# Moving the transposes of layer 1's rows from TensorE to 32x32 block transposes on VectorE

## The chip, the cores and the metric

The kernel runs on one core of one Trainium2 chip. The metric is the device time of that core in microseconds (us), from the first instruction to the last, as a median over several executions. Engines are named as the profile names them: PE is TensorE (PEld its weight loads), DVE is VectorE, ACT is ScalarE, POOL is GpSimd, SPq the DMA queue that SyncE feeds.

## The reference, cut to what matters

The input x has 16 batch elements of 1024 rows and 256 channels in float32. Two graph layers follow each other.

```python
def _batchnorm(x, gamma, beta):                      # over all 16 x 1024 rows
    return (x - mean(x, 0)) * rsqrt(var(x, 0) + EPS) * gamma + beta

# layer 0: aggregation over the graph, a two-layer perceptron with two batch norms
out = relu(_batchnorm(agg @ W1.T + b1, g1, be1)) @ W2.T + b2
x = _layernorm(x + _batchnorm(out, g2, be2))
# layer 1: a graph gate makes q; k and v are linear; 4 heads of 64 channels
attn = softmax(einsum('bhnd,bhmd->bhnm', q, k) * scale)
x = _layernorm(x + einsum('bhnm,bhmd->bhnd', attn, v))
```

The second batch norm needs the statistics of all rows, so its input (called y) goes to DRAM. It comes back when layer 1 begins with a batch element. The kernel computes y with channels on partitions; the residual and the layer norm want rows on partitions. Somewhere y must be transposed.

## The kernel before

Layer 1 is a software pipeline. While the scores, exponentials and weighted sums of one batch element run, the rows of later ones are prepared in small pieces, a pair of 128-row tiles (b, j) at a time: load, batch norm (`bn2`), transpose with residual and statistics (`ln1_a`), normalization (`ln1_b`), transpose of the result (`x1_t`).

```python
def fetch_rows(b, j):
    nc.sync.dma_start(yts[b, j], yT_dram[b][:, :, ts(j, 2 * P)])
    nc.sync.dma_start(xrs[b, j], x[b, ts(j, 2 * P), :].rearrange("(a p) c -> p a c", p=P))
...
def bn2(b, j):
    for c in range(CT):
        t = yts[b, j][:, c, :]
        nc.scalar.activation(t, t, AF.Identity, bias=t2[:, c : c + 1], scale=s2[:, c : c + 1])
...
def ln1_a(b, j):
    p = ps_t.tile([P, 2, C], F32, tag="t", name="py")
    for a in range(2):
        for c in range(CT):
            nc.tensor.transpose(p[:, a, ts(c, P)], yts[b, j][:, c, ts(a, P)], ident)
    x1s[b, j] = x1p.tile([P, 2, C], F32, tag="x1", name=f"x1_{b}_{j}")
    nc.vector.tensor_add(x1s[b, j], p, xrs[b, j])
    mvs[b, j] = ln_stats(sm, x1s[b, j], f"a{b}_{j}")
```

VectorE also adds up the exponentials (`sums`). When all are in, TensorE sums the result over partitions into the denominators of the softmax (`dens`, tile pd):

```python
def sums(g):
    ...
        for a in range(2):
            nc.vector.tensor_add(ACC[b, hf, pair], ACC[b, hf, pair], E[g, a])
def dens(b, hf):
    p = ps_t.tile([P, FB], F32, tag="t", name="pd")
    for pair in range(NP):
        acc = ACC.pop((b, hf, pair))
        for h in range(2):
            k = 32 * (2 * pair + h)
            nc.tensor.matmul(p[k : k + 32, :], ones32, acc[:, h, :], start=True, stop=True)
```

A small scheduler puts each piece into a half-bundle (`put`), and `arrange` orders the pieces of a half-bundle. The denominators and the batch norm come first there:

```python
order = (dens, recips, finish_a, finish_b, x1_t, ln1_a, ln1_b, means, load, crow)
short = (dens, recips, finish_a, x1_t, ln1_a, crow)
def arrange(pieces):
    first = [fa for fa in pieces if fa[0] is dens]
    ...
    first += [fa for fa in pieces if fa[0] is bn2]
    ...
    return first + flat
```

One period of this pipeline is one batch element: two halves (hf) of two head pairs each, so four bundles of pieces, each followed by four steps of scores and sums.

## Time and profile before

| what | before |
|---|---|
| time, median of 4 executions | 2586.84 us |
| TensorE busy in the profiled execution | 2514.0 of 2584.4 us (97%) |
| TensorE waits of pd for VectorE's sums | 2.6 us in 9 |
| TensorE waits of the scores for an exponential | 19.6 us in 16 |
| transposes that the change removes | 60 groups of four, 0.43 us each |

A row of the view of waits names an engine and a line of the kernel, what it waited for, and then the total in us, the number of waits and the longest.

```profile
PE s L686 <- ACT e L698: 19.6, 16, 4.1
...
PE pd L738 <- DVE acc L707: 2.6, 9, 0.3
```

In the timeline the columns are start, duration, engine, line, operation, output and inputs, count.

```profile
1333.86 7.89 DVE L707 TENSOR_TENSOR acc<-acc,e 128x1024 f32<-128x1024 f32 x6
```

Six sums take 7.9 us when nothing disturbs them.

### The profile page before, as it was taken

How to read it: one execution, taken by the hardware profiler on the slowest of the kernel's cores; microseconds unless marked ns; L12 is line 12 of the kernel's file. 1: busy time of each engine (PE TensorE's matmuls, PEld its weight loads, DVE VectorE, ACT ScalarE, POOL GpSimd, SP SyncE). 2: the span in 40 equal slices, each digit the busy share in tenths (PEclk: the TensorE clock that was granted, in tenths of full speed). 3: DMA queues.
4: the chain of work that ended last, by engine and by line, in shares of the span. 5: the costliest groups of instructions: out<-in, count | busy, mean ns of one | idle time of the engine just before them, and what ended most of it. 6: DMA issues, size and time to landing. Idle time of an engine off the chain costs nothing.

```text
span 2584.4 us, 33296 instructions
## 1 busy us (share of the span) xinstructions
PE 2514.0 (97%) x13053; PEld 1092.5 (42%) x13053; DVE 1650.8 (64%) x2588; ACT 1135.0 (44%) x1509; POOL 565.7 (22%) x588
## 2 busy tenths in 40 slices
PE   8999999998997999999999999999999999999997
PEld 4444444443443544344444444444444444443432
DVE  5555555456676676675766757666576675766666
ACT  2000000004543656465564655646556465564644
POOL 2222222223654011011110111201121110211112
PEclk9999999999998999999999999999999999999998
DMA  3122221230873101101011010110101100010000
GB/s 130 73 90 82 98 98 66 98 130 30 329 302 129 41 21 54 34 25 34 29 54 34 25 33 30 54 33 25 34 25 58 34 25 34 25 53 22 9 9 26
DMA packets 94115, 163.77 MB, mean 63 GB/s; under 512 B 7688, under 2 KB 73856, under 8 KB 86784
## 3 DMA queue, kind: packets, MB, share of 16 engines
q1 hardware_dynamic: 93952, 161.57, 17.8%
q8 instruction: 105, 1.72, 0.3%
q14 instruction: 58, 0.48, 0.1%
HBM read 98.58 MB, written 62.98 MB: 63 GB/s over the span
## 4 chain that ended last, share of the span: by engine, by line
PE 87%; ACT 7%; DVE 3%; issue 1%; DMA 1%; POOL 0%; SPq 0%; DVEq 0%; ACTq 0%; POOLq 0%
PE s L686 15%; PE o L717 15%; PE pg L660 14%; PE pa L295 14%; PE po L457 7%; PE ph L326 7%; PE pk L635 4%; PE pv L646 2%; DVE acc L707 2%; PE pd L738 1%; ACT e L698 1%; PE px L585 1%; PE pa L276 1%; ACT wg L623 1%; ACT wg L622 1%
## 5 line engine op out<-in xcount | busy, mean ns | idle before, releaser
L698 ACT ACTIVATE e<-s 128x1024 f32<-128x1024 f32 x512 | 496.0, 1020 | 378.1 <-PE s L686 331.1
L707 DVE TENSOR_TENSOR acc<-acc,e 128x1024 f32<-128x1024 f32 x384 | 470.7, 1226 | 94.5 <-ACT e L698 66.3
L686 PE MATMUL s<-qT,kT 64*64 64x512 f32 x4096 | 491.6, 595 | 20.3 <-ACT e L698 19.6
L717 PE MATMUL o<-e,v 64*64 64x512 f32 x4096 | 486.1, 590 | 0.0
L660 PE MATMUL pg<-wg,x 128*128 128x512 f32 x960 | 437.6, 593 | 0.0
L686 PEld LDWEIGHTS s<-qT,kT 64*64 64x64 f32 x4096 | 147.0, 133 | 315.3 <-issue 252.1
L717 PEld LDWEIGHTS o<-e,v 64*64 64x64 f32 x4096 | 156.9, 133 | 284.2 <-issue 278.6
L66 POOL TENSOR_SCALAR rs_z<-mv_z 128x2 f32<-128x2 f32 x64 | 41.0, 641 | 1046.1 <-DVE mv_z L519 963.2
L627 DVE SCALAR_TENSOR_TENSOR wg<-wg,adj_sb 128x1024 f32<-128x1024 f32 x128 | 156.8, 1225 | 127.6 <-ACT wg L623 125.4
L660 PEld LDWEIGHTS pg<-wg,x 128*128 128x128 f32 x960 | 170.1, 190 | 159.2 <-issue 159.1
L93 ACT COPY u<-pa 128x512 f32<-128x512 f32 x15 | 8.8, 585 | 475.3 <-PE pa L295 475.3
L295 PE MATMUL pa<-AhT,x 128*128 128x512 f32 x360 | 161.8, 592 | 0.0
L668 DVE TENSOR_TENSOR qT<-pg,para_sb 128x512 f32<-128x512 f32 x64 | 44.2, 691 | 168.0 <-PE pg L660 167.0
L66 POOL TENSOR_SCALAR rs_a<-mv_a 128x2 f32<-128x2 f32 x64 | 43.0, 671 | 415.3 <-DVE mv_a L519 413.9
L586 ACT COPY x1T<-px 128x512 f32<-128x512 f32 x64 | 37.1, 581 | 202.5 <-PE px L585 202.5
L646 PE MATMUL pv<-kvw,x1T 128*128 128x256 f32 x512 | 120.1, 379 | 0.0
L635 PE MATMUL pk<-x1T,kvw 128*128 128x512 f32 x256 | 118.9, 609 | 0.7 <-ACT x1T L586 0.7
L326 PE MATMUL ph<-agg,SW 128*128 128x512 f32 x240 | 112.8, 592 | 0.0
L729 DVE TENSOR_TENSOR ot<-o,ot 128x512 f32<-128x512 f32 x64 | 44.1, 689 | 102.3 <-ACT ot L728 102.3
L295 PE MATMUL pa<-T,sx 128*128 128x512 f32 x240 | 107.9, 592 | 0.0
L295 PEld LDWEIGHTS pa<-AhT,x 128*128 128x128 f32 x360 | 68.4, 190 | 86.1 <-issue 86.1
L646 PEld LDWEIGHTS pv<-kvw,x1T 128*128 128x128 f32 x512 | 94.0, 190 | 17.9 <-issue 7.4
(188 smaller groups left out, 3258.1 us busy)
## 6 DMA issues: line engine op xcount, KB each, us to landing
h<-hT SPq DMA_DIRECT2D x28, 1024.0 KB, 4.4
hL<-h SPq DMA_DIRECT2D x28, 1024.0 KB, 9.8
x<-in_x_dram SPq DMA_DIRECT2D x16, 1024.0 KB, 7.3
yT<-y SPq DMA_DIRECT2D x32, 512.0 KB, 3.2
out_dram<-r SPq DMA_DIRECT2D x64, 256.0 KB, 2.1
yt<-yT SPq DMA_DIRECT2D x62, 256.0 KB, 3.4
xr<-in_x_dram SPq DMA_DIRECT2D x62, 256.0 KB, 5.0
crow<-crow_d SPq DMA_DIRECT2D x15, 512.0 KB, 4.1
```

The lines of the kernel that those rows point to most:

```text
L66: nc.gpsimd.tensor_scalar(dst, src, add, None, op0=OP.add)
L295: nc.tensor.matmul(p, xs[n][:, k, :], bs[n][:, k, :], start=(k == 0), stop=(k == KN - 1))
L326: nc.tensor.matmul(p, ws[n][:, ts(f, P)], bs[n], start=True, stop=True)
L457: nc.tensor.matmul(p, ws[n][:, k, :], bs[n][:, k, :], start=(k == 0), stop=(k == KF - 1))
L627: nc.vector.scalar_tensor_tensor(t, t, 1.0, adj_sb[:, i, :], op0=OP.add, op1=OP.mult)
L635: nc.tensor.matmul(p, kvw[:, k, ts(c, P)], x1Ts[b][:, k, ts(h, FB)], start=(k == 0), stop=(k == CT - 1))
L646: nc.tensor.matmul(p[:, ts(a, C)], x1Ts[b][:, k, ts(j + a, P)], kvw[:, k, C:], start=(k == 0), stop=(k == CT - 1),)
L660: nc.tensor.matmul(pg[b], x1s[b, k // 2][:, k % 2, ts(c, P)], wgs[b, k][:, ts(h, FB)], start=(k == 0), stop=(k == NT - 1))
L686: nc.tensor.matmul(t[r * HD : (r + 1) * HD, h, :], kTs[b, pair][h * HD : (h + 1) * HD, ts(2 * cb + r, HD)], qTs[b, pair, hf][h * HD : (h + ...
L698: nc.scalar.activation(E[g, a], S.pop((g, a)), AF.Exp)
L707: nc.vector.tensor_add(ACC[b, hf, pair], ACC[b, hf, pair], E[g, a])
L717: nc.tensor.matmul(O[b, hf, pair][r][h * HD : (h + 1) * HD, :], vs[b][r * HD : (r + 1) * HD, cb, pair * P + h * HD : pair * P + (h + 1) * HD],
```

## The change

Its intent: take the transposes, 1% of TensorE's work, away from the engine that bounds the kernel. y is laid out in DRAM so that a DMA can fetch 32x32 blocks, already put where they belong as blocks; VectorE's block transpose then turns each block. Batch norm now needs a different constant for each block of columns, and goes with the residual to GpSimd, which is idle for 78% of the span (busy 565.7 of 2584.4 us). Batch element 0 keeps the old way.

```diff
+    Q = 32
+    NQ = P // Q
+    y_blk = [yT_all[b].rearrange("i (d e) (q n) -> q e (i d) n", e=Q, q=NQ) for b in range(B)]
...
         def fetch_rows(b, j):
-            nc.sync.dma_start(yts[b, j], yT_dram[b][:, :, ts(j, 2 * P)])
+            if b == 0:
...
+            else:
+                for q in range(NQ):
+                    nc.sync.dma_start(
+                        yts[b, j][q * Q : (q + 1) * Q].rearrange("p a (d n) -> p (a d) n", n=Q),
+                        y_blk[b][q][:, ts(j, 2 * C // Q), :],
+                    )
...
+        def bn2_q(b, j):
+            y = yts[b, j].rearrange("p a (d n) -> p a d n", n=Q)
+            for k, op in enumerate((OP.mult, OP.add)):
+                sc = stq[:, k, :].unsqueeze(1).unsqueeze(3).to_broadcast([P, 2, C // Q, Q])
+                nc.gpsimd.tensor_tensor(y, y, sc, op)
+
+        def rows(b, j):
+            x1s[b, j] = x1p.tile([P, 2, C], F32, tag="x1", name=f"x1_{b}_{j}")
+            nc.vector.transpose(x1s[b, j].rearrange("p a c -> p (a c)"), yts[b, j].rearrange("p a c -> p (a c)"))
+            nc.gpsimd.tensor_add(x1s[b, j], x1s[b, j], xrs[b, j])
...
-                put(b - 2, j + 1, bn2, b, j)
+                put(b - 2, j + 1, bn2_q, b, j)
+                put(b - 2, j + 2, rows, b, j)
                 put(b - 2, j + 2, ln1_a, b, j)
...
-        order = (dens, recips, finish_a, finish_b, x1_t, ln1_a, ln1_b, means, load, crow)
+        order = (dens, recips, finish_a, rows, finish_b, x1_t, ln1_b, ln1_a, means, load, crow)
-        short = (dens, recips, finish_a, x1_t, ln1_a, crow)
+        short = (dens, recips, finish_a, x1_t, crow)
```

For b > 0 `ln1_a` now holds the statistics alone. Cut here: the new layout's stores, the round trip of the constants through DRAM into `stq`, a buffer count of 5 instead of 6 for small tiles, and the kernel's fallback path.

More of the change, by code (lines that the diff above doesn't have):

```diff
@@ L75, in load_vec @@
         return t
-    yT_all = dram.tile([B, P, CT, N], F32, name="yT")
-    yT_dram = [yT_all[b] for b in range(B)]
+    yT_all = dram.tile([B, NT, C, P], F32, name="yT")
+    y_chunk = [[yT_all[b][:, ts(c, P), :].rearrange("i p n -> p i n") for c in range(CT)] for b in range(B)]
+    Q = 32
+    NQ = P // Q
+    y_blk = [yT_all[b].rearrange("i (d e) (q n) -> q e (i d) n", e=Q, q=NQ) for b in range(B)]
+    st2_dram = dram.tile([2, C], F32, name="st2_d")
     c_dram = [dram.tile([NT, P], F32, name=f"crow_d{b}") for b in range(B)]
@@ L390, in gnn_norm_attention_kernel @@
         ones32 = keep.tile([P, 32], F32, name="ones32")
+        stq = keep.tile([P, 2, C // Q], F32, name="stq")
         nc.gpsimd.memset(ones32, 1.0)
@@ L409, in load @@
         def load(b, j):
-            yts[b, j] = ldp.tile([P, CT, 2 * P], F32, tag="yt", name=f"yt{b}_{j}")
+            shape = [P, CT, 2 * P] if b == 0 else [P, 2, C]
+            yts[b, j] = ldp.tile(shape, F32, tag="yt", name=f"yt{b}_{j}")
             xrs[b, j] = ldp.tile([P, 2, C], F32, tag="xr", name=f"xr{b}_{j}")
@@ L414, in fetch_rows @@
         def fetch_rows(b, j):
-            nc.sync.dma_start(yts[b, j], yT_dram[b][:, :, ts(j, 2 * P)])
+            if b == 0:
+                for c in range(CT):
+                    nc.sync.dma_start(
+                        yts[b, j][:, c, :].rearrange("p (a n) -> p a n", n=P), y_chunk[b][c][:, ts(j, 2), :]
+                    )
+            else:
+                for q in range(NQ):
+                    nc.sync.dma_start(
+                        yts[b, j][q * Q : (q + 1) * Q].rearrange("p a (d n) -> p (a d) n", n=Q),
+                        y_blk[b][q][:, ts(j, 2 * C // Q), :],
+                    )
             nc.sync.dma_start(xrs[b, j], x[b, ts(j, 2 * P), :].rearrange("(a p) c -> p a c", p=P))
@@ L474, in second @@
                     if k >= 5:
-                        nc.sync.dma_start(yT_dram[b][:, :, ts(k - 5, FB)], ys[k - 5])
+                        for c in range(CT):
+                            nc.sync.dma_start(
+                                y_chunk[b][c][:, ts(k - 5, FB // P), :],
+                                ys[k - 5][:, c, :].rearrange("p (i n) -> p i n", n=P),
+                            )
                         if k == 6:
@@ L538, in fast @@
         otp = pool("otp", 3)
-        sm = pool("sm", 6)
+        sm = pool("sm", 5)
         rp = pool("rp", 2)
@@ L552, in bn2, with constants_q @@
                 nc.scalar.activation(t, t, AF.Identity, bias=t2[:, c : c + 1], scale=s2[:, c : c + 1])
+        def constants_q():
+            with nc.allow_non_contiguous_dma(reason="a few hundred numbers"):
+                for k, t in enumerate((s2, t2)):
+                    nc.sync.dma_start(st2_dram[k].rearrange("(k p) -> p k", p=P), t)
+                for q in range(NQ):
+                    nc.sync.dma_start(
+                        stq[q * Q : (q + 1) * Q], st2_dram.rearrange("s (d e) -> e s d", e=Q)
+                    )
+        def bn2_q(b, j):
[7 more added lines that the diff above has]
+            nc.gpsimd.tensor_add(x1s[b, j], x1s[b, j], xrs[b, j])
         def begin(b):
@@ L558, in ln1_a @@
         def ln1_a(b, j):
-            p = ps_t.tile([P, 2, C], F32, tag="t", name="py")
-            for a in range(2):
-                for c in range(CT):
-                    nc.tensor.transpose(p[:, a, ts(c, P)], yts[b, j][:, c, ts(a, P)], ident)
-            x1s[b, j] = x1p.tile([P, 2, C], F32, tag="x1", name=f"x1_{b}_{j}")
-            nc.vector.tensor_add(x1s[b, j], p, xrs[b, j])
+            if b == 0:
+                p = ps_t.tile([P, 2, C], F32, tag="t", name="py")
+                for a in range(2):
+                    for c in range(CT):
+                        nc.tensor.transpose(p[:, a, ts(c, P)], yts[b, j][:, c, ts(a, P)], ident)
+                x1s[b, j] = x1p.tile([P, 2, C], F32, tag="x1", name=f"x1_{b}_{j}")
+                nc.vector.tensor_add(x1s[b, j], p, xrs[b, j])
             mvs[b, j] = ln_stats(sm, x1s[b, j], f"a{b}_{j}")
@@ L888, in arrange @@
             many = [fa for fa in pieces if fa[0] in long]
-            first += [fa for fa in pieces if fa[0] is bn2]
+            first += [fa for fa in pieces if fa[0] is bn2_q]
             few = [fa for fa in pieces if fa not in first + gate + many]
@@ L952, in fast @@
         begin(0)
+        constants_q()
         for f in (bn2, ln1_a):
@@ L1026, in general @@
         yt = one.tile([P, CT, N], F32, name="g_yt")
-        nc.sync.dma_start(yt, yT_all[bass.ds(b, 1)].rearrange("o p c n -> p (o c) n"))
+        for c in range(CT):
+            nc.sync.dma_start(
+                yt[:, c, :].rearrange("p (i n) -> p i n", n=P),
+                yT_all[bass.ds(b, 1), :, ts(c, P), :].rearrange("o i p n -> p (o i) n"),
+            )
         x1 = one.tile([P, NT, C], F32, name="g_x1")
```

## The prediction

> **What bounds the kernel now.** I read the page's busy table first, then the busy time of each engine in stretches of 100 us, then the timeline of one full period of layer 1 (one batch element, 1299 to 1406 us; it repeats 14 times with the changed part in it; it is made of four bundles of small pieces, each followed by four steps of scores, exponentials and weighted sums), and last the stretches where GpSimd and VectorE work at once.
>
> ```profile
> PE 2514.0 (97%) x13053; PEld 1092.5 (42%) x13053; DVE 1650.8 (64%) x2588; ACT 1135.0 (44%) x1509; POOL 565.7 (22%) x588
> ```
>
> TensorE is the bound. By stretches it is busy 98.6 to 98.9 us of every 100 between 880 and 2380 us, at a granted clock of 1.00, so only what it no longer has to do, or a wait given to it, moves the time. The transposes that go are the group py:
>
> ```profile
> 1344.80 0.60 PE L562 MATMUL py<-ident,yt 128*128 128x128 f32 x4
> 1345.23 2.31 PE L660 MATMUL pg<-wg,x 128*128 128x512 f32 x5
> ```
>
> Four transposes show 0.60 us of (overlapped) busy time, but the next matmul starts 0.43 us after the first of them. 0.43 us is what one group occupies, not four times the 272 ns that the tile view gives for one.
>
> The second thing is where VectorE, idle a third of the time on average, is late. That is where its sums of exponentials feed the denominators (pd) at the head of the third bundle of the period:
>
> ```profile
> 1357.23 7.87 DVE L707 TENSOR_TENSOR acc<-acc,e 128x1024 f32<-128x1024 f32 x6
> ...
> 1363.81 1.05 PE L738 MATMUL pd<-acc,ones 128*32 128x512 f32 x4
> ...
> 1365.16 1.05 PE L738 MATMUL pd<-acc,ones 128*32 128x512 f32 x4 [0.29 <-DVE acc L707]
> ```
>
> TensorE's second four wait for VectorE's last sum, which ends at 1365.1 us. From 1341.7 us to there the timeline shows VectorE with about 0.6 us of gaps. So in this stretch of 23 us VectorE has no slack: whatever delays it there stops TensorE one for one. Elsewhere in the period it has slack (4.57 us and 5.13 us of waiting before qT). The other denominators, at 1314 us, are not tight: the sums end at 1311.9 us.
>
> The third thing is what a large GpSimd operation does to VectorE:
>
> ```profile
> 620.43 2.34 POOL L469 TENSOR_TENSOR hT<-hT,hT 128x1024 f32<-128x1024 f32 x1 [4.78 <-DVE hT L451]
> 620.48 3.38 DVE L451 TENSOR_TENSOR hT<-hT 128x1024 f32<-128x1024 f32 x1 [0.18 <-ACT hT L443]
> ```
>
> The same VectorE subtraction has a median of 1214 ns in the other 14 cases. Here it took 3.38 us: it began 0.05 us after GpSimd's 2.34 us addition and ended 1.09 us after it. [...]
>
> [...] the reciprocal root's two-column step on GpSimd took 1.71 us at 1332.80 beside VectorE's gate product, against a minimum of 713 ns. [...] here 1266 ns for 128x512 against 692 ns, 1.8 times. [...] the new pieces have 128 B. The only small pieces here, 2304 of 4 B for the layer-0 vectors, were all in place some 7 us after the first issue, and landed within 4.7 us at most.
>
> **The change part by part.** Batch elements 1 to 15, four row pairs each: 60 pairs.
>
> TensorE: minus 60 groups of 0.43 us, minus 26 us (1.0%), if nothing else happens.
>
> ScalarE: minus 120 activations of 589 ns, 71 us. It is not the bound. It removes at most one 0.87 us wait per period (scores behind an exponential at 1353.30), 12 us in all, if that stretch were not governed by VectorE.
>
> VectorE: minus 60 additions out of PSUM at 684 ns, plus 60 block transposes at an estimated 0.65 us: neutral in busy time. But the statistics that follow now wait for GpSimd.
>
> GpSimd: plus two broadcast operations and one addition of 128x512 per pair, 3 x 1.27 = 3.8 us, 15.2 us per period, 228 us in all. It was busy 15 to 18 us of 100, so it has room. [...]
>
> DMA: a row load goes from 256 pieces of 1 KB to 2048 of 128 B in four transfers. The last is issued about 1.65 us after the first (0.55 us each) and landings took 3.4 us, so I estimate 5 to 6 us where it was 3.4. It is mostly hidden, because GpSimd is later still. The stores of y in 512 B instead of 2 KB runs fall where DMA is 78% busy and TensorE 100%: I count nothing. The round trip of the constants happens once, in the opening: a few us at most, hidden.
>
> Now the tight stretch, from the end of the first bundle through the second to the denominators, with the program order of the new code:
>
> (a) GpSimd's two operations for pair 1 come after the output norm's small ones, about 1336.5 us, in the middle of six back-to-back sums (1333.9 to 1341.7). [...] up to +2.5.
>
> (b) Pair 0: VectorE transposes, GpSimd adds, VectorE takes statistics. GpSimd must first finish the four small operations of the preceding output norm, some 2.5 us beside VectorE's sum, then add for 1.27. VectorE, done with its transpose, stands still for about 3 us.
>
> (c) Pair 1: between the two statistics GpSimd has to do the root (1.0), two operations for pair 2 (2.5) and the addition (1.3), 4.8 us. VectorE has two gate products, a bit operation, a transpose and two normalizations, also about 4.8[...], about +3.7.
>
> (d) Two operations for pair 3 fall into the six sums before the denominators: up to +2.5.
>
> The sum is up to 11.7 us per period. Not every collision will happen in full (an operation can fall into a gap that (b) or (c) opens), so I take 7.5. The end of the stretch moves by 7.5; the two groups removed inside it gain nothing, since VectorE ends it; the two removed behind it give 0.87. That is +6.6 us per period, times 14 periods: +93. The opening, where TensorE has long waits on ScalarE and VectorE keeps slack, gains about its four groups, -2. Sum +91 us: about 2677 us.
>
> **The rivals.** First, the plain gain: GpSimd's work hides and the 26 us come out, perhaps with the 0.87 us waits: 2548 to 2560 us. For it: GpSimd has 80% idle time, VectorE a third. The author moved statistics behind the previous pair's normalization, and VectorE's first sum before the transpose, which gives GpSimd time. Against it: the 23 us without gaps and the 0.29 us wait. Second, only the direct waits (b) and (c) count, in part, about 4 us per period, [...] small GpSimd operations never lengthened a sum (384 of them, at most 1252 ns): +3.1 x 14 = +44, about 2628 us. Third, the DMA pieces are slow: if a load took over 10 us, GpSimd would stand at pair 2 and hold the addition of pair 1 and so VectorE, a further 3 to 5 us per period: 2720 to 2750 us. The 4 B pieces speak against it. Fourth, GpSimd's column-broadcast operand could be slower than a plain one; each 0.3 us on it adds about 1 us per period in (c) and (d), +15.
>
> **Range and chances.** 2675 us, between the second rival and the full sum (11.7 - 0.9 = 10.8 per period, +151, 2737). Range 2605 to 2750. Faster by over 2% (below 2535) would need more than everything TensorE can gain: 0.02. Within 2% (up to 2638) is the second rival or better: 0.28. Slower: 0.70.
>
> **What would show it.** In the new profile: the transposes gone and TensorE's share down to 93 or 94%; a wait of pd on acc of 5 to 12 us once per period instead of 0.29; VectorE's statistics of x waiting for GpSimd's addition, some 3 us, twice per period in the second bundle; sums stretched from 1.22 us to as much as 2.5 us next to a GpSimd operation; yt landing in 4 to 6 us; the block transpose near 0.65 us. It would be wrong if the pd waits stay under 1 us (then the first rival), if sums never stretch [...], if GpSimd waits for the DMA rather than for VectorE (the third), or if the block transpose takes over 1 us.

Some of its figures are estimates. The 0.65 us of the block transpose are taken from VectorE's 512-column additions, 672 to 692 ns in the profile before. The terms (a), (c) and (d) take it that where a large GpSimd operation and a VectorE operation run at once, one is held up for about the length of the other, 1.27 us for 128x512 on GpSimd. In the profile before the one subtraction of 3.38 us (1214 ns in the median of the others) speaks for it; that it is so each time was not shown. The 1266 and 692 ns are an operation with two inputs of 128x512 on GpSimd and on VectorE.

## The result and the profile after

The changed kernel takes 2696.44 us (median of 4 executions, 2694.0 to 2699.37) where the kernel before takes 2586.84 (2585.6 to 2589.86). The ratio is 1.0422, with a 95% interval of 1.0404 to 1.044: slower. Ratios in this document are the mean time of one kernel's fast runs over the mean of the other's in the same rounds, so they are not quite the ratio of the medians.

The busy table of the changed kernel, and its row of DMA issues (after the size of one: us from issue to landing):

```profile
PE 2519.2 (94%) x12813; PEld 1082.6 (40%) x12813; DVE 1752.5 (65%) x2588; ACT 1081.1 (40%) x1389; POOL 882.6 (33%) x768
...
yt<-yT SPq DMA_DIRECT2D x240, 64.0 KB, 3.1
```

TensorE has 240 matmuls fewer, yet it is busy for 5.2 us longer. That is the first thing to explain. The second is in the view of waits:

```profile
POOL yt L591 <- DMA yt<-yT: 174.0, 17, 12.9
...
PE pd L783 <- DVE acc L752: 87.1, 14, 6.7
...
DVE st_a L539 <- POOL x L596: 49.9, 31, 2.2
...
PE s L731 <- ACT e L743: 37.7, 15, 4.2
```

The wait for VectorE's sums has gone from 2.6 to 87.1 us, in 14 pieces of some 6 us, one in each period. VectorE waits 49.9 us for GpSimd's residual addition, a wait that did not exist before. (The 174 us of GpSimd for its DMA are the first row pair of each period; whether they matter is for an experiment.)

One period of the changed kernel (its first denominators start at 1344.41 us), in the timeline of VectorE and GpSimd. Lines: 752 sums, 595 block transpose, 596 residual, 539 statistics, 591 batch norm, 616 normalization.

```profile
1364.15 9.35 DVE L752 TENSOR_TENSOR acc<-acc,e 128x1024 f32<-128x1024 f32 x6
1366.73 3.03 POOL L591 TENSOR_TENSOR yt<-yt,stq 128x512 f32<-128x512 f32 x2
...
1377.66 0.70 DVE L595 STREAM_TRANSPOSE x<-yt 128x512 f32<-128x512 f32 x1
...
1379.18 1.27 POOL L596 TENSOR_TENSOR x<-x,xr 128x512 f32<-128x512 f32 x1
1380.49 0.43 DVE L539 BATCH_NORM_STATS2 st_a<-x 128x6 f32<-128x256 f32 x1 [2.12 <-POOL x L596]
...
1385.18 2.23 POOL L591 TENSOR_TENSOR yt<-yt,stq 128x512 f32<-128x512 f32 x2
1385.24 1.27 DVE L616 SCALAR_TENSOR_TENSOR x<-x,mv_a,rs_a 128x256 f32<-128x256 f32 x1
1386.44 1.26 DVE L616 SCALAR_TENSOR_TENSOR x<-x,mv_a,rs_a 128x256 f32<-128x256 f32 x1
...
1388.86 0.43 DVE L539 BATCH_NORM_STATS2 st_a<-x 128x6 f32<-128x256 f32 x1 [1.16 <-POOL x L596]
...
1392.92 9.18 DVE L752 TENSOR_TENSOR acc<-acc,e 128x1024 f32<-128x1024 f32 x6
1393.56 3.48 POOL L591 TENSOR_TENSOR yt<-yt,stq 128x512 f32<-128x512 f32 x2
```

There are two kinds of loss. Where VectorE needs GpSimd's result, it stands still: 2.12 and 1.16 us, in brackets. Where both work at once on unrelated data, both are slow: six sums take 9.35 and 9.18 us instead of 7.9, two normalizations 1.27 and 1.26 us where the median before was 479 ns, and GpSimd's own pairs of operations 2.23 to 3.48 us where one alone takes 1.04 us at the least.

TensorE at the end of that stretch:

```profile
1384.24 2.01 PE L731 MATMUL s<-qT,kT 64*64 64x512 f32 x16 [2.40 <-ACT e L743]
...
1402.15 1.92 PE L783 MATMUL pd<-acc,ones 128*32 128x512 f32 x4 [6.34 <-DVE acc L752]
...
1404.92 6.94 PE L705 MATMUL pg<-wg,x 128*128 128x512 f32 x14
```

It waits 6.34 us. Then its four matmuls of pd take 1.92 us; in the prediction's lines four take 1.05. The next stretches of 2 us show why (columns: stretch, its length, busy us and instructions of PE, PEld, DVE, ACT and POOL, granted clock, DMA share, GB/s):

```profile
1402.00:1404.00 2.00, 1.84 (x4) 0.19 (x4) 2.00 (x6) 0.00 (x0) 0.55 (x1) 0.50 0.05 12
1404.00:1406.00 2.00, 2.00 (x8) 1.48 (x7) 1.94 (x5) 1.17 (x2) 0.82 (x1) 0.50 0.00 0
1406.00:1408.00 2.00, 2.00 (x5) 0.84 (x5) 0.18 (x1) 0.00 (x0) 0.93 (x2) 0.89 0.01 4
1408.00:1410.00 2.00, 2.00 (x6) 0.80 (x6) 0.68 (x1) 0.00 (x0) 0.00 (x0) 1.00 0.00 0
```

The granted clock (1.00 is full speed) is 0.50 for about 4 us after the wait. TensorE stopped at 1395.8 us; the clock is 0.91 in the mean of 1398 to 1400 us and 0.50 from 1400 on, and it is back at 1.00 from 1408 on. From how long a wait on the clock falls was not shown: after two waits of 2.40 us it fell in one kernel and not in another (see e5). So this wait of 6.34 us costs its length and then about 2 us of slow matmuls (some 4 us at a clock of 0.50).

**The account.** Over the whole span TensorE's time is its busy time plus its waits. From the profiled executions, in us (waits under 1 us in all are given as 0; the last column is in e5 the wait of the transposed denominators for their copy, 2.1 us in the other kernels of the table, and in e10 and e11 that of pd for another addition; in e10 the graph matmuls wait 7.9 us besides):

| kernel | span | PE busy | pd waits for acc | scores wait for e | other waits that changed |
|---|---|---|---|---|---|
| before | 2584.4 | 2514.0 | 2.6 | 19.6 | |
| after | 2693.9 | 2519.2 | 87.1 | 37.7 | |
| e1_before_delay | 2708.7 | 2545.8 | 95.9 | 20.0 | |
| e3_no_bn | 2603.6 | 2497.9 | 36.8 | 18.6 | |
| e5_late_dens | 2601.1 | 2503.0 | 0 | 37.7 | 12.7 |
| e6_add_dve | 2653.5 | 2516.7 | 47.1 | 41.1 | |
| e7_no_pool | 2673.0 | 2511.0 | 0 | 112.3 | |
| e9_detached2 | 2634.4 | 2504.2 | 40.9 | 37.7 | |
| e10_tuned | 2598.2 | 2496.1 | 0 | 14.7 | 28.2 |
| e11_tuned_add_dve | 2555.6 | 2477.5 | 0 | 14.7 | 14.0 |
| e12_before_tuned | 2578.9 | 2503.1 | 0 | 27.7 | |

From before to after: pd +84.5, scores +18.1, busy +5.2, together +107.8 of the 109.5 by which the span grew. The busy time is itself a difference: 60 groups of 0.43 us, 26 us, went, and 31 us came by the slow clock.

### The profile page after: what moved, and what is told of

Its sections match the earlier page's. It is cut to its first block, busy times and chain, and to the rows that moved or that the text cites. A ratio compares the mean times of both kernels' runs of the same rounds, so it can differ in the third digit from the quotient of the medians.

```text
span 2693.9 us, 33329 instructions
## 1 busy us (share of the span) xinstructions
PE 2519.2 (94%) x12813; PEld 1082.6 (40%) x12813; DVE 1752.5 (65%) x2588; ACT 1081.1 (40%) x1389; POOL 882.6 (33%) x768
## 4 chain that ended last, share of the span: by engine, by line
PE 79%; DVE 11%; POOL 5%; ACT 2%; issue 2%; DMA 0%; POOLq 0%; SPq 0%; DVEq 0%; ACTq 0%
PE pg L705 14%; PE pa L300 13%; PE s L731 13%; PE o L762 13%; PE po L474 7%; PE ph L331 7%; DVE acc L752 4%; PE pk L680 4%; PE pv L691 2%; PE pd L783 2%; POOL x L596 1%; PE px L630 1%; DVE wg L672 1%; POOL yt L591 1%; PE pa L281 1%
## 5 line engine op out<-in xcount | busy, mean ns | idle before, releaser
L752 DVE TENSOR_TENSOR acc<-acc,e 128x1024 f32<-128x1024 f32 x384 | 517.4, 1347 | 70.6 <-ACT e L743 39.6
L731 PE MATMUL s<-qT,kT 64*64 64x512 f32 x4096 | 492.1, 595 | 39.5 <-ACT e L743 37.7
L705 PE MATMUL pg<-wg,x 128*128 128x512 f32 x960 | 444.0, 605 | 0.0
L66 POOL TENSOR_SCALAR rs_z<-mv_z 128x2 f32<-128x2 f32 x64 | 53.2, 831 | 849.9 <-DVE mv_z L540 680.5
L705 PEld LDWEIGHTS pg<-wg,x 128*128 128x128 f32 x960 | 179.2, 197 | 180.0 <-issue 178.9
L591 POOL TENSOR_TENSOR yt<-yt,stq 128x512 f32<-128x512 f32 x120 | 168.7, 1405 | 182.1 <-DMA yt<-yT 174.0
L783 PE MATMUL pd<-acc,ones 128*32 128x512 f32 x256 | 60.3, 697 | 87.1 <-DVE acc L752 87.1
L596 POOL TENSOR_TENSOR x<-x,xr 128x512 f32<-128x512 f32 x60 | 82.9, 1381 | 131.8 <-issue 83.9
L616 DVE SCALAR_TENSOR_TENSOR x<-x,mv_a,rs_a 128x256 f32<-128x256 f32 x120 | 105.9, 918 | 2.7 <-POOL rs_a L68 2.7
```

Source lines behind the costliest of these rows:

```text
L591: nc.gpsimd.tensor_tensor(y, y, sc, op)
L705: nc.tensor.matmul(pg[b], x1s[b, k // 2][:, k % 2, ts(c, P)], wgs[b, k][:, ts(h, FB)], start=(k == 0), stop=(k == NT - 1))
L731: nc.tensor.matmul(t[r * HD : (r + 1) * HD, h, :], kTs[b, pair][h * HD : (h + 1) * HD, ts(2 * cb + r, HD)], qTs[b, pair, hf][h * HD : (h + ...
```

## The experiments

The theory after the result: VectorE is late by some 7 us per period at the denominators, half because it needs GpSimd's residual, half because its operations are slower beside GpSimd's other work (six sums 9.35 and 9.18 us instead of 7.9); TensorE loses that, and then its clock (0.50 for some 4 us). Rivals: the small DMA pieces; a mere wait for data; the new order of pieces; something in the transposes themselves.

### e1: delay VectorE in the kernel before

Nothing of the change, only lateness: five operations that change nothing (the maximum of the sum with itself) after the last sum of the pair whose denominators were tight.

```diff
...
+ if k == g + NK - 1 and (hf_, pair_) == (0, 1):
+     acc_ = ACC[bb, hf_, pair_]
+     for _ in range(5):
+         nc.vector.tensor_tensor(acc_, acc_, acc_, OP.max)
```

> The kernel before with five more VectorE operations (maximum of the sum with itself, about 1.22 us each, 6.1 us) put after the last sum that feeds the first denominators of each of the 16 batch elements; nothing else changed, result still right. Theory (VectorE has no slack in this stretch, its delay goes to TensorE one for one): 16 x 6.1 = +98 us; with the halved clock that the changed kernel shows for about 4 us after each such wait (about 2.2 us lost), a further 35 us: about 2720 us, and 2685 us if the slow clock does not come with the wait. Rival (VectorE is idle a third of the time, so the delay is caught up): below 2610 us.

Measured: 2710.27 us, ratio 1.048 (1.0463 to 1.0497), correct. TensorE of this kernel, in the view of waits and in the timeline of one period:

```profile
PE pd L738 <- DVE acc L1010: 95.9, 16, 6.6
```

```profile
1402.67 1.92 PE L738 MATMUL pd<-acc,ones 128*32 128x512 f32 x4 [6.58 <-DVE acc L1010]
```

The delay goes to TensorE almost one for one: five operations in each of 16 periods are 97.7 us of VectorE work, and the wait grows by 93.3, to 95.9 us. And again four matmuls take 1.92 us after it (clock 0.50 from 1402.6 to 1404.6 us and 0.64 in the 2 us that follow); TensorE's busy time grew by 31.8 us with exactly the same matmuls. 93.3 us of wait and 31.8 of slow clock make 125 us; the time grew by 124. So lateness at this one place is enough for all of the loss, and the slow clock adds a third to it. (The delay sits directly before the denominators; that a delay further up in the stretch arrives in full is not tested by it.)

### e3: no batch norm on GpSimd

```diff
-                nc.gpsimd.tensor_tensor(y, y, sc, op)
+                pass
...
-            nc.gpsimd.tensor_add(x1s[b, j], x1s[b, j], xrs[b, j])
+            nc.gpsimd.tensor_add(x1s[b, j], xrs[b, j], xrs[b, j])
```

The result is wrong; adding x to itself keeps the numbers in range. The addition still waits for the transpose's buffer and VectorE still waits for the addition.

> The changed kernel without the two broadcast operations on GpSimd; the addition stays, but adds the x rows to themselves to keep the numbers finite (wrong result on purpose). Theory: the lengthened sums (1.5 and 1.3 us per period), the lengthened normalizations (1.6) and part of the second wait go, the first wait of about 2 us stays: minus 66 us and up to 31 us more from the clock, 2600 to 2630 us. Rival, direct waits alone: 2680 us or so.

Measured: 2605.74 us, ratio 1.0076 (1.0057 to 1.0095). In the timeline of this kernel:

```profile
1335.59 7.89 DVE L752 TENSOR_TENSOR acc<-acc,e 128x1024 f32<-128x1024 f32 x6
...
1350.22 0.43 DVE L539 BATCH_NORM_STATS2 st_a<-x 128x6 f32<-128x256 f32 x1 [1.88 <-POOL x L596]
...
1360.62 7.87 DVE L752 TENSOR_TENSOR acc<-acc,e 128x1024 f32<-128x1024 f32 x6
```

Both runs of sums are back at exactly their old length, so it was the batch norm's operations, on data that has nothing to do with the sums, that stretched them. Of the two waits for the residual the first stays (1.88 us) and the second goes (26.8 us in 15 waits where the change has 49.9 in 31). pd still waits 36.8 us in all, up to 3.1 us. That the time fell by 91 us is the account at work: pd 50.3, scores 19.1, busy time 21.3.

### e4: the rows in 512-byte pieces

Two plain transfers of 512-byte pieces instead of four of 128-byte pieces. The result is wrong, as the blocks lie in the wrong places; the addition takes x twice, as in e3, to keep the numbers in range.

```diff
-                for q in range(NQ):
-                    nc.sync.dma_start(... y_blk[b][q][:, ts(j, 2 * C // Q), :])
+                for c in range(CT):
+                    nc.sync.dma_start(... y_chunk[b][c][:, ts(j, 2), :])
...
-            nc.gpsimd.tensor_add(x1s[b, j], x1s[b, j], xrs[b, j])
+            nc.gpsimd.tensor_add(x1s[b, j], xrs[b, j], xrs[b, j])
```

> The changed kernel with the rows fetched in pieces of 512 B by two transfers instead of 128 B blocks by four; all work on the engines stays, the addition adds the x rows to themselves (wrong result on purpose). Theory: the DMA's pieces cost nothing on the path: 2685 to 2700 us. Rival (GpSimd waits 174 us in all for yt, so the small pieces are what is paid): 2640 us or less.

Measured: 2695.79 us, ratio 1.042 (1.0403 to 1.0437), against 2696.44 and 1.0422 for the change. pd still waits 80.1 us, and GpSimd still waits 165.4 us for its DMA (174.0 before). So the small pieces cost nothing that reaches the end, and GpSimd's wait for the first load of a period is time in which nobody needs GpSimd. The DMA rival falls.

### e2 and e9: GpSimd's addition detached

e2 let GpSimd add into the other buffer (`xrs` instead of `x1s`), so that VectorE would not wait for it.

```diff
-            nc.gpsimd.tensor_add(x1s[b, j], x1s[b, j], xrs[b, j])
+            nc.gpsimd.tensor_add(xrs[b, j], x1s[b, j], xrs[b, j])
```

> The changed kernel with GpSimd's addition written into the x rows' own buffer, which nothing reads: VectorE's statistics no longer wait for GpSimd, every GpSimd operation stays (wrong result on purpose: the residual is missing). Theory of two parts (direct waits 2.1 + 1.2 us per period[...]): minus 3.3 x 14 = 46 us, 2650 us, down to 2620 us if the shorter waits also spare the slow clock; denominators' wait from 6.3 to about 3 us. Rival, collisions alone: 2685 to 2697 us. Rival, direct waits alone: 2560 to 2590 us.

It took 10340.17 us and gave a correct result. The kernel checks the range of its scores and has a slow general path for those that are out of range. Without the residual the general path ran: its tiles fill the trace. This run says nothing on the question. e9 repeats it with numbers in range: VectorE transposes x instead of y. The result is wrong, and y's buffer comes free somewhat earlier than in the change, which is an impurity.

```diff
-            nc.vector.transpose(... x1s[b, j] ..., yts[b, j] ...)
-            nc.gpsimd.tensor_add(x1s[b, j], x1s[b, j], xrs[b, j])
+            nc.vector.transpose(... x1s[b, j] ..., xrs[b, j] ...)
+            nc.gpsimd.tensor_add(xrs[b, j], x1s[b, j], xrs[b, j])
```

> The detached addition again, mended: the first try left the scores without their range, so the kernel's own fallback ran. VectorE now transposes the x rows, and GpSimd's addition goes into the x rows' buffer that nothing reads later; every GpSimd operation stays, no statistic waits for one (wrong result on purpose). Theory of two parts: minus 3.3 us per period of direct waits, 2650 us, down to 2620 us if the shorter wait spares some of the slow clock. [...] Rival, direct waits alone: 2590 us or less.

Measured: 2637.06 us, ratio 1.0193 (1.0176 to 1.021). GpSimd does all its work, nobody waits for its result, and still pd waits 40.9 us:

```profile
1377.43 1.38 PE L783 MATMUL pd<-acc,ones 128*32 128x512 f32 x4 [3.44 <-DVE acc L752]
```

With e3 this splits the 87.1 us of pd: 36.8 us remain with the first wait for the result and without the batch norm, 40.9 us with the collisions and without that wait; together 77.7. It is not a strict sum, as e3 keeps the addition on GpSimd and both edits shift the order of things, but neither kind alone makes the loss. Theories with one cause only would have put e9 at the change's time or at the full gain; it is between.

### e5: ask for the denominators later

If the loss is VectorE's lateness at one place, TensorE should be given other work there. The denominators of half 0 move from the head of the third bundle's first half to its end:

```diff
+            last_ = [fa for fa in pieces if fa[0] is dens and fa[1][1] == 0]
+            pieces = [fa for fa in pieces if fa not in last_]
...
-            return first + flat
+            return first + flat + last_
```

> The changed kernel with the first denominators moved from the head of the third bundle to the end of its first half, behind one group of transposes and seven graph matmuls, some 3.4 us of TensorE work; result right. Theory: the wait of 6.3 us per period shrinks by 3.4 to about 2.9: minus 14 x 3.4 = 48 us, 2650 us, or 2620 us if the slow clock goes too. Rival (VectorE or GpSimd is simply too slow over the period, and the wait moves elsewhere): 2685 us or more.

Measured: 2603.0 us, ratio 1.0056 (1.0039 to 1.0073), correct. TensorE of this kernel in the same place of a period:

```profile
1356.91 2.66 PE L731 MATMUL s<-qT,kT 64*64 64x512 f32 x16 [2.40 <-ACT e L743]
1359.33 3.00 PE L762 MATMUL o<-e,v 64*64 64x512 f32 x16
...
1369.62 6.17 PE L705 MATMUL pg<-wg,x 128*128 128x512 f32 x14
1375.72 1.06 PE L783 MATMUL pd<-acc,ones 128*32 128x512 f32 x8
1377.49 0.65 PE L794 MATMUL pr<-ident,dt 128*128 128x128 f32 x4 [0.71 <-ACT dt L785]
```

The pd wait is gone, better than expected. GpSimd, VectorE, the DMA and the transposes do the same work as in the change; 93 of its 110 us go with the order of one matmul group. What is left is a wait of the scores (37.7 us), one behind the denominators (12.7 us where it was 2.1; the 0.71 above), and some slow clock: the two groups after the 2.40 us wait take 2.66 and 3.00 us where 1.90 is usual (clock 0.50 from 1359 to 1361 us). After a wait of the same 2.40 us the changed kernel's scores ran at full clock (2.01 us, clock 1.00 from 1384 to 1388 us).

### e6: the residual on VectorE

```diff
-            nc.gpsimd.tensor_add(x1s[b, j], x1s[b, j], xrs[b, j])
+            nc.vector.tensor_add(x1s[b, j], x1s[b, j], xrs[b, j])
```

> The changed kernel with the residual addition on VectorE behind its transpose; the two broadcast operations stay on GpSimd; result right. Theory: the waits for GpSimd's addition (3.3 us per period in the tight stretch) go, 2 x 0.69 us of VectorE work comes: about minus 1.9 x 14 = 27 us, 2670 us, with 2645 us if the clock gains too. Rival, direct waits are the whole cost: 2600 us or less. Rival, collisions alone: 2700 to 2715 us.

Measured: 2653.84 us, ratio 1.0246 (1.0227 to 1.0265), correct. pd waits 47.1 us instead of 87.1: giving VectorE 60 more operations makes it earlier, because it no longer waits for GpSimd. The collisions with the batch norm stay: six sums still take 9.36 and 9.18 us.

### e7 and e8: nothing on GpSimd

Batch norm in eight pieces on ScalarE (each block of columns has its own constants), the residual on VectorE; e8 adds e5's later denominators.

```diff
...
+            for d in range(C // Q):
+                t = yts[b, j][:, :, ts(d, Q)]
+                nc.scalar.activation(t, t, AF.Identity, bias=stq[:, 1, d : d + 1], scale=stq[:, 0, d : d + 1])
...
```

> The changed kernel with the batch norm on ScalarE, eight pieces of 64 columns a pair, and the residual addition on VectorE: no large GpSimd operation is left; result right. Theory: VectorE's delay in the tight stretch falls to its two extra additions, 1.4 us per period[...]: 2590 to 2630 us. Rival (the block transposes or the DMA are the cost, not GpSimd): 2670 us or more.

> As the run without large GpSimd operations, and the first denominators later. Theory: no wait of the denominators is left, the 26 us of the removed transposes come out except what ScalarE's pieces cost: 2560 to 2600 us, so possibly faster than the kernel before. Rival: ScalarE's pieces hold up the exponentials by some 3 us per period: 2610 to 2640 us.

Both missed: 2672.0 us (1.0324, 1.0307 to 1.0341) and 2688.8 us (1.0388, 1.0371 to 1.0406), correct. By the time alone e7 would speak for the rival, that transposes or DMA are to blame. Its timeline, VectorE's sums, ScalarE and then TensorE, speaks otherwise:

```profile
1357.51 7.89 DVE L751 TENSOR_TENSOR acc<-acc,e 128x1024 f32<-128x1024 f32 x6
...
1375.07 2.76 ACT L590 ACTIVATE yt<-yt,stq 128x64 f32<-128x64 f32 x8 [2.77 <-DMA yt<-yT]
...
1382.93 3.40 PE L730 MATMUL s<-qT,kT 64*64 64x512 f32 x16 [7.96 <-ACT e L742]
```

Six sums take 7.89 us again, and the longest of all 384 takes 1.25, so without GpSimd's large operations nothing stretches them. That pd does not wait at all shows less: TensorE comes to it after a wait of 7.96 us, and VectorE itself had to wait for the last exponentials, so a lateness of VectorE had no chance to show. The loss is on ScalarE. In its order the eight pieces come before the exponential: it stands 2.77 us before the rows have come, then works 2.76 us on the pieces, and the exponential behind them is late. The scores wait 112.3 us in all. I had put a piece lower, an estimate that no run had shown; one takes 423 to 444 ns (they overlap, so eight take 2.76 us). In e8 there is no pd wait for the later denominators to remove, and they add 10.6 us of the wait behind them and 5.5 us of busy time. These two moved the wait to another engine; they do not contradict the theory, and they do show what the batch norm on ScalarE costs in this form.

### e10 to e12: a tuned order, with and without the change

e10 keeps all work of the change and moves three pieces: denominators late as in e5, the reciprocals behind two graph matmuls, and the output norm's last step (`finish_b`) to the end of its half-bundle. The reason for the last is ScalarE's timeline in the changed kernel:

```profile
1379.02 1.09 ACT L826 ACTIVATE r<-r,nm,rs_z 128x256 f32<-128x256 f32 x2 [2.51 <-POOL nm L818]
```

ScalarE waits 2.51 us for a small GpSimd operation (nm) of the output norm, and the exponential behind it is the one that the scores then wait 2.40 us for. e11 adds e6's edit. e12 is the control: the three moves in the kernel before.

```diff
+            last_ = [fa for fa in pieces if fa[0] is finish_b or (fa[0] is dens and fa[1][1] == 0)]
+            pieces = [fa for fa in pieces if fa not in last_]
...
+            if flat and flat[0][0] is recips and flat[0][1][1] == 0 and all(fa[0] is graph for fa in flat[1:3]):
+                flat = flat[1:3] + flat[:1] + flat[3:]
-            return first + flat
+            return first + flat + last_
```

> The changed kernel with three moves in the order alone: the first denominators at the end of the first half of the third bundle, the reciprocals' transposes two graph matmuls later (0.71 us wait of them for ScalarE's copy), and the closing normalization on ScalarE last in its half bundle (so the exponential is not behind its 2.5 us wait for GpSimd). Theory: the denominators' wait stays away (2603 us), minus 14 x (0.7 + up to 2.4) us: 2560 to 2595 us, equal to the kernel before or up to 1% faster. Rival (VectorE's lateness only moves on): 2600 us or more.

> The same three moves with the residual addition on VectorE. Theory: with the denominators out of the way VectorE has the slack, so it is within 10 us of the run with the three moves, 2560 to 2595 us. If VectorE still bounds a stretch, whichever of the two loads it less there is faster.

> Control: the same three moves on the kernel before. It waits 0.29 us for the sums, about 0.3 us of starting gap and 0.87 us for an exponential per period: at most minus 16 x 1.3 = 20 us, likely 2570 to 2587 us. What the change is worth in the new order is its run against this one.

Measured, all correct: e10 2598.99 us (1.0044, 1.0029 to 1.0059), e11 2555.89 us (0.9877, 0.9861 to 0.9894), e12 2580.37 us (0.997, 0.9956 to 0.9984). e10 missed its range by 4 us: the wait of the scores fell to 14.7 us as meant, but pd now waits 28.2 us for the last addition of the weighted sums (ot) on VectorE:

```profile
1376.39 1.68 PE L783 MATMUL pd<-acc,ones 128*32 128x512 f32 x8 [2.14 <-DVE ot L774]
```

With the residual on VectorE that wait is half as long:

```profile
1360.78 1.06 PE L783 MATMUL pd<-acc,ones 128*32 128x512 f32 x8 [1.08 <-DVE ot L774]
```

I had expected e11 within 10 us of e10 and not below 2560 us; it is 43 us faster than e10, of which 14.2 us are the wait itself, 7.9 a wait of the graph matmuls (pg) in e10 that e11 no longer has, and 18.6 TensorE's busy time, the clock that falls less (1.06 instead of 1.68 us for eight matmuls; from 1100 to 1500 us the mean clock is 1.00 in e11 and 0.99 in e10). The busy tables of e11 and of the control e12:

```profile
PE 2477.5 (97%) x12813; PEld 1066.4 (42%) x12813; DVE 1766.0 (69%) x2648; ACT 1079.7 (42%) x1389; POOL 801.6 (31%) x708
```

```profile
PE 2503.1 (97%) x13053; PEld 1090.3 (42%) x13053; DVE 1651.7 (64%) x2588; ACT 1134.5 (44%) x1509; POOL 571.6 (22%) x588
```

TensorE's busy time differs by 25.6 us, the times by 24.5 (e11 waits 13.0 us less at the scores and 14.0 more at pd, which cancel). These are the transposes: the 26 us that the change was to gain are there, once the order makes room for GpSimd. e11 beats both kernels, the one before by 1.2%. The interval lies clear of 1.

## Why the prediction was right or wrong

It said 2675 us, within 2605 to 2750, and slower; 2696.44 came. The place of the loss and the two ways in which VectorE becomes late were right. That the number came so near is in part luck: a lateness somewhat too large, reached by a guessed discount, stands against a slow clock that the sum did not have.

- **TensorE loses 26 us of work.** Right: e11 against e12 shows 25.6 us. In the change itself it is hidden by the slow clock. (Its reading that TensorE is busy for 98.6 to 98.9 us of every 100 holds for the stretches it looked at; over all from 880 to 2380 us it is 98.4 to 100.0.)
- **VectorE without slack before one pair of denominators, and each delay there one for one on TensorE.** Right for the end of the stretch, and shown apart from the change by e1, and by e5, which removes only the demand. The reading of about 0.6 us of gaps was low: VectorE is busy for 21.64 of the 23.4 us from 1341.7, and 0.83 us of the rest is one wait for ScalarE, before its gate product at 1345.71.
- **How late VectorE becomes.** Right in size. Measured from the head of the period's first denominators (1314.12 before, 1344.41 after) to VectorE's last sum (1365.10, 1402.10), the stretch grew from 50.98 to 57.69 us, by 6.7; the prediction took 7.5.
- **The four terms.** Each was too large. (a) was up to 2.5: 9.35 less 7.89 is 1.46. (b) was about 3: 2.12. (c) was 3.7: 1.16 of wait and two normalizations longer by some 0.8 each, 2.7. (d) was up to 2.5: 9.18 less 7.87 is 1.31. They add to 7.6, of which 6.7 arrive at the end of the stretch. The other 0.9 fits VectorE's own idle time: 1.76 us before, and from 1373.42 to 1402.10 after, without the two waits for GpSimd, 0.86; the prediction had 11.7 and a guessed discount. That (a) and (d) come from GpSimd's batch norm is shown by e3 (without it 7.89 and 7.87 us), that (b) comes from the awaited addition by e9 and e6. VectorE pays less than GpSimd's whole operation, and GpSimd pays a part: its two operations beside the sums took 3.03 and 3.48 us, not 2 x 1.04.
- **From lateness to time.** Here a term was missing: "+6.6 us per period, times 14 periods: +93" counts the wait and nothing after it. The waits measure 84.5 us at pd, but each is followed by some 4 us at half clock: 31 us in all. Both waits (102.6 us) less the 26 us of the transposes come to 77 us, below the predicted 91; the clock makes that up and goes 17 beyond. e1 shows the same 32 us without anything of the change.
- **The wait of the scores.** The prediction let ScalarE's lighter load remove up to 0.87 us per period. Instead it grew, 19.6 to 37.7 us: ScalarE waits for small GpSimd operations of the output norm and passes it on. They are late, not slow: from the first to the end of nm they take 2.34 us before (from 1344.97) and 2.49 after (from 1376.73). Their input comes late from VectorE, which the stretched sums of (a) have held up, and TensorE, with two groups of transposes less, reaches the scores 0.88 us sooner. In e3, without transposes and without the batch norm, the wait is 18.6 us, so it comes with the batch norm on GpSimd. The prediction charged (a) at pd alone; it is paid at the scores too.
- **What would show it.** TensorE at 94% (predicted 93 or 94); pd waits of 6 us once per period (5 to 12); sums up to 2.04 us (up to 2.5); block transpose 0.70 us (0.65). The statistics' wait was said to be some 3 us twice; it was 2.12 and 1.16.
- **The rivals.** The plain gain did not come as the change stands. "Only direct waits" falls by e3 and e9. The prediction named a sign for the slow DMA, GpSimd waiting for it, and that sign came, 174.0 us; but the slow DMA falls by e4, and from the first of four issues at 1329.96 to GpSimd's start at 1335.09 there are 5.1 us, within the 5 to 6 estimated. The slow broadcast operand is the other way round: 1.04 us at the least and 1.11 in the median, against 1.27 and 1.39 for two full operands. The new order of the pieces and the block transposes were not tested alone. The four terms leave nothing of the lateness for them, and e11 has both of them and the small DMA pieces and still gains what the transposes cost.

What stays open: how much of (c) is the slower normalizations (1.27 and 1.26 us) and how much GpSimd's own lateness was not taken apart.

## What to carry to other kernels

An idle engine is no free place for work if its result is awaited, or if its operations stretch those of an engine that has no slack at some point of the period (here 49.9 us of waits for GpSimd's addition, and six sums in 9.35 us instead of 7.89): look for that point before moving work. Count the slow clock after a wait on TensorE as well as the wait: here, after waits of some 6 us, it was a third more (31.8 us on 93.3 in e1). And when a change that takes real work off the bound is slower, move the demand as well as the work: the same change with three pieces reordered and the residual kept on VectorE was 1.2% faster than the kernel before.
